# Moving weight loads, a half chunk's split and LayerNorm statistics to other steps of a planned two-layer kernel

## The chip, the cores and the metric

The kernel runs on one core of a Trainium2 chip (trn2). The metric is the device time of one execution in microseconds. A core has five engines that run side by side, each in its own order: TensorE (PE; its weight loads are shown apart as PEld), VectorE (DVE), ScalarE (ACT), GpSimd (POOL) and SyncE (SP), whose queue issues nearly all DMAs here.

## The reference

Two feed-forward layers with 4-bit weights stand around a long convolution (an S4 layer); each is added to its input.

```python
x = x + 0.5 * ffn(layernorm(x))
x = x + s4(layernorm(x))          # causal convolution over the last axis, plus D * u
x = x + 0.5 * ffn(layernorm(x))
# layernorm: (x - mean) / sqrt(var + 1e-5) over the last axis
# ffn: h = silu(x @ Wg) * (x @ Wu); return h @ Wd
# W[k, n] = scales[k // 128, n] * (w4[k, n] - (z4[k // 128, n] + 1)), eight 4-bit values to an int32
```

x is 2 x 1024 x 1024 in float32, so 2048 rows of 1024. The hidden width of the feed-forward layers is 2752, which is 21 chunks of 128 and a half chunk of 64.

## The kernel before, in words

**Jobs.** The 2048 rows are four blocks of 512 (four tiles of 128 rows each). A job is one feed-forward layer on one block, so there are eight, in the order `JOBS = [(0, 1), (1, 1), (0, 3), (1, 3), (2, 1), (3, 1), (2, 3), (3, 3)]`: block, then 1 for the first layer and 3 for the second. The convolution of a block (its LayerNorm has the number 2) is done during the up stage of the job that follows the block's first layer: in jobs 1, 2, 5 and 6. The block's next norm (number 3) follows there too.

**Stages and steps.** Each job has an up stage and a down stage. The up stage (`gate_up`, L727) multiplies the normalized, transposed rows with gate and up weights in eight waves of three or two chunks (the last wave has the half chunk as well), each wave over eight groups of 128 rows of weights: 64 steps, with 12, 8 or 10 matmuls (L753). Each product stays in a PSUM accumulator that is rescaled in place between two groups (`scaled`, L721 to L725), half of them by ScalarE and half by VectorE; after the last group `gated` (L778) makes silu(gate) * up, and GpSimd splits the result into a high and a low part (L785, L787). The down stage (`down`, L814) has two passes over 22 chunks: 44 steps of 8 matmuls (L825), with the same kind of rescaling; the last chunk of a pass, steps 21 and 43, is the half chunk, with 4. In job 0 ScalarE takes three of the four rescalings in every second down step. `back` (L843) then transposes the result and adds it to x, one half of the columns (512) at a time: the first half during the down stage, the second half in steps 0 to 3 of the next job's up stage.

**Weights.** In job 0 the 4-bit weights are turned into bytes first. For wave w, `fetch` and `fetch_zeros` load packed words and zero points (four DMAs of 128 or 192 KB, eight for the last wave, L514 and L521), `split` (L582) makes signed bytes in six VectorE operations (L575, L577, L579), and `dequantize` (L605) copies them in eight pieces on GpSimd (L608), each written to DRAM by a DMA (L609). All later steps load bytes from there, four steps ahead of their use (`load_bytes`, L685), and a cast three steps ahead turns them into matmul weights (`make_weights`: GpSimd L701, in job 0 for three steps of eight ScalarE L699). A wave's first load needs all eight writes of that wave. `first_weights` (L643) fixes at which steps of job 0 all of this is written.

**Order.** `fast` (L1420) writes the program job by job. Work that lies beside the matmuls is hung on steps: `at(up, s, f)` or `at(dn, d, f)` calls f at the start of a step, after the loads and casts of that step and before its matmuls. The framework's planner then orders each engine's instructions at compile time, and may run what is ready earlier than it was written. `in_order_of_writing(f, engines)` (L141) takes that freedom away: each instruction that f writes for the named engines is put behind the one written before it on that engine. `in_pieces` (L587) hangs a generator's pieces on a list of steps, with VectorE in order of writing.

**Norms.** `moments` (L176) runs BATCH_NORM_STATS2 on each half row (L187), an aggregate for each of four tiles (L190), and `guess` (L194, three small operations, a first value for 1/sqrt). `moments_by_tile` is the same as a generator: with `halves=True` a piece is one statistic, or one statistic with its aggregate, and the ninth is the guess. `deviations` (L206) refines with Newton's formula in ten small operations:

```python
for three in (3.0, 12.0, 768.0):
    nc.vector.tensor_tensor(e, r, r, ALU.mult)
    nc.vector.tensor_tensor(e, e, ve, ALU.mult)
    nc.vector.scalar_tensor_tensor(r, e, three, r, ALU.subtract, ALU.mult)
nc.vector.tensor_scalar(r, r, -factor / 8192, None, ALU.mult)
```

For job 1's rows this happens in the down stage of job 0: statistics pinned to steps 4 to 20, Newton to 21, normalization (L256) from 22 and turning (`turn_by_pool`, L236: transposes, a copy on ScalarE, a cast and a subtraction on GpSimd) from 24. For the norms 2 and 3 in jobs 1, 2, 5 and 6, `moments` and `deviations` are hung on single steps without an order: steps 4 and 5, and 27 and 28 (61 and 62 in job 1).

**The half chunk.** `gated_half` (L790) writes the high part of h (L802) and the low part (L804) of the 64-wide chunk. In jobs 1 to 7 GpSimd does this at down steps 1 and 2. In job 0 VectorE does it at once, at the end of the up stage.

## Time and profile before

| what | value |
|---|---|
| median of 3 runs | 2098.28 us (2097.29 to 2102.04) |
| the profiled execution: its time, and its span in the trace | 2097.59 us, 2095.8 us |
| TensorE busy, VectorE, ScalarE, GpSimd | 98%, 80%, 67%, 62% |
| granted TensorE clock | 0.998 |
| job 0, up stage and down stage | 176.7 us, 91.1 us |
| job 1, up stage and down stage | 193.0 us, 82.2 us |
| jobs 2, 5, 6, up stage | 188.3, 186.8, 186.8 us |
| jobs 3, 4, 7, up stage | 158.2, 158.3, 157.7 us |
| jobs 2 to 6, down stage | 80.5 to 80.6 us |

A stage's time is from its first matmul's start to the next stage's first, in the timeline of TensorE. All jobs have the same matmuls; the up stages of jobs 1, 2, 5 and 6 have the convolution's besides. In the lines of a timeline the columns are start in us, duration in us, engine, line of the program, operation, tiles written and read, their shapes, and the number of like instructions merged; in brackets stands the idle time before, and what ended it. In the chain of work that ended last they are start, duration, engine, tile and line. In a table of windows they are the window and its length, then the busy time of each engine with its number of instructions, the granted clock, the share of the DMA engines' time, and GB/s.

### The profile page before, as it was taken

Reading aid. Unit: us, or ns where it says so; the run is one execution under the profiler, and the core shown is the slowest. Engines: PE = TensorE matmul, PEld = TensorE weight load, DVE = VectorE, ACT = ScalarE, POOL = GpSimd, SP = SyncE. Lnnn points to the kernel's source line nnn. Section 1 sums busy time; section 2 is a strip of 40 time slices with the busy share of each in tenths; the row PEclk is TensorE's granted clock in tenths of the full one; section 3 lists DMA queues with packets and bytes.
Section 4 is the critical chain, followed back from the end, with each engine's and each line's share of the span. In section 5 each row is a group of like instructions: output and inputs, shape, how many; then the busy total and the mean of one; then the engine's idle time right before and its main releaser. Section 6 shows DMA issues by size and latency. Waiting matters only on the chain.

```text
span 2095.8 us, 30242 instructions
## 1 busy us (share of the span) xinstructions
PE 2054.6 (98%) x9556; PEld 1410.6 (67%) x9556; DVE 1671.5 (80%) x2749; ACT 1398.9 (67%) x2185; POOL 1291.6 (62%) x1688
## 2 busy tenths in 40 slices
PE   6999999999999999999999999999999999999998
PEld 4555775677776578655876568675686766866576
DVE  8888887778888877797778878878788787777776
ACT  6777777746655776667667776547765467667775
POOL 5867758657754577555955568455684546845542
PEclk9999999999999999999999999999999999999999
DMA  4324321113411126211441124111151111531111
GB/s 144 119 85 146 111 66 54 36 56 74 110 39 55 32 53 170 72 31 36 122 137 37 31 51 126 44 51 32 46 130 37 51 39 35 133 128 36 33 35 60
DMA packets 239719, 151.03 MB, mean 72 GB/s; under 512 B 98747, under 2 KB 226596, under 8 KB 239550
## 3 DMA queue, kind: packets, MB, share of 16 engines
q1 hardware_dynamic: 238246, 146.60, 24.7%
q8 instruction: 78, 1.28, 0.3%
q10 hardware_dynamic: 1016, 1.82, 0.2%
q14 instruction: 91, 0.75, 0.1%
q0 software_dynamic: 288, 0.59, 0.1%
HBM read 104.45 MB, written 25.50 MB: 62 GB/s over the span
## 4 chain that ended last, share of the span: by engine, by line
PE 92%; DVE 4%; DMA 1%; ACT 1%; issue 1%; POOL 0%; SPq 0%; ACTq 0%; DVEq 0%; POOLq 0%
PE pg L753 56%; PE po L825 29%; PE pc L1151 3%; PE pb L847 1%; PE pb L1151 1%; DVE pg L725 1%; PE st L230 1%; DMA b<-wq 1%; ACT g L780 0%; DVE po L725 0%; DVE x L256 0%; DMA x<-in_L_attn_u_dram 0%; POOL q L608 0%; DVE hf L783 0%; PE pt L230 0%
## 5 line engine op out<-in xcount | busy, mean ns | idle before, releaser
L723 ACT ACTIVATE pg<-pg,rat 128x512 f32<-128x512 f32 x1240 | 787.5, 661 | 418.1 <-PE pg L753 415.9
L725 DVE TENSOR_TENSOR pg<-pg,rat 128x512 f32<-128x512 f32 x1168 | 776.6, 693 | 159.3 <-PE pg L753 153.4
L753 PE MATMUL pg<-xTh,w_up 128*128 128x512 f32 x2752 | 840.5, 435 | 1.1 <-DVE pg L725 0.7
L753 PE MATMUL pg<-xTl,w_up 128*128 128x512 f16 x2752 | 716.7, 382 | 11.6 <-DVE pg L725 5.6
L701 POOL CAST w_up<-b 128x768 fp32r<-128x768 int8 (+2 forms) x490 | 378.0, 777 | 504.6 <-PE pg L753 405.7
L753 PEld LDWEIGHTS pg<-xTh,w_up 128*128 128x128 f32 x2752 | 518.3, 189 | 175.9 <-DVE pg L725 12.2
L723 ACT ACTIVATE po<-po,ratd 128x512 f32<-128x512 f32 x660 | 431.8, 661 | 164.7 <-PE po L825 164.1
L825 PE MATMUL po<-hl,w_down 128*128 128x512 f32 x1344 | 530.5, 397 | 3.7 <-DVE po L725 3.6
L825 PE MATMUL po<-hh,w_down 128*128 128x512 f32 x1344 | 521.2, 390 | 0.0
L725 DVE TENSOR_TENSOR po<-po,ratd 128x512 f32<-128x512 f32 x620 | 430.4, 698 | 113.3 <-PE po L825 109.1
L753 PEld LDWEIGHTS <-w_up 128*128 128x128 bf16 x2752 | 228.4, 99 | 330.3 <-issue 151.0
L701 POOL CAST w_down<-bd 128x512 fp32r<-128x512 int8 x352 | 218.4, 624 | 158.5 <-PE po L825 90.4
L825 PEld LDWEIGHTS po<-hl,w_down 128*128 128x128 f32 x1344 | 251.2, 188 | 73.3 <-DVE po L725 12.2
L825 PEld LDWEIGHTS po<-hh,w_down 128*128 128x128 f32 x1344 | 252.6, 188 | 49.0
L787 POOL TENSOR_TENSOR hl<-hf,hh 128x512 fp32r<-128x512 f32 x168 | 217.9, 1297 | 8.0
L783 DVE SCALAR_TENSOR_TENSOR hf<-pg,rat,g 128x512 f32<-128x512 f32 x168 | 123.2, 749 | 49.3 <-ACT g L780 40.4
L780 ACT ACTIVATE g<-pg,rat 128x512 f32<-128x512 f32 x168 | 111.0, 687 | 48.5 <-PE pg L753 32.8
L785 POOL CAST hh<-hf 128x512 fp32r<-128x512 f32 x168 | 106.1, 632 | 55.0 <-PE pg L753 31.0
L282 POOL TENSOR_TENSOR lo<-x,hi 128x512 f16<-128x512 f32 x48 | 62.2, 1296 | 0.0
L187 DVE BATCH_NORM_STATS2 stats<-x 128x6 f32<-128x512 f32 x88 | 60.0, 682 | 0.5
L280 POOL TENSOR_TENSOR mid<-hi,top 128x512 bf16<-128x512 f32 x48 | 56.4, 1174 | 0.0
L296 POOL TENSOR_TENSOR xTh<-turned 128x512 fp32r<-128x512 bf16 x48 | 55.9, 1165 | 0.0
(216 smaller groups left out, 1104.2 us busy)
## 6 DMA issues: line engine op xcount, KB each, us to landing
b<-wq SPq DMA_DIRECT2D x319, 96.0 KB
bd<-wdq SPq DMA_DIRECT2D x336, 64.0 KB
x<-in_L_attn_u_dram SPq DMA_DIRECT2D x30, 512.0 KB
b<-wq SPq DMA_DIRECT2D x128, 64.0 KB
xs<-x SPq DMA_DIRECT2D x16, 512.0 KB
x<-xs SPq DMA_DIRECT2D x16, 512.0 KB
out_dram<-x SPq DMA_DIRECT2D x12, 512.0 KB
b<-wq SPq DMA_DIRECT2D x64, 80.0 KB
```

Source lines behind the costliest of these rows:

```text
L187: nc.vector.bn_stats(stats[:, t, i, :], x[b][t][:, bass.ts(i, 512)])
L282: nc.gpsimd.tensor_tensor(lo[:, own], n[:, own], hi[:, own].bitcast(F32), ALU.subtract)
L701: nc.gpsimd.tensor_copy(t, b)
L723: nc.scalar.activation(dst, src, AF.Copy, scale=sc)
L725: nc.vector.tensor_tensor(dst, src, sc.to_broadcast([P, TB]), ALU.mult)
L753: nc.tensor.matmul(p, weights, (lo, hi)[k][:, g, :], start=(g == 0 and not done), stop=(g == GK - 1 and done), skip_group_check=True,)
L780: nc.scalar.activation(g, pg, AF.Silu, scale=rat[:, 2 * f, GK - 1 :])
L783: nc.vector.scalar_tensor_tensor(hf, pu, last, g, ALU.mult, ALU.mult)
L785: nc.gpsimd.tensor_copy(hi, hf)
L787: nc.gpsimd.tensor_tensor(lo, hf, hi.bitcast(F32), ALU.subtract)
L825: nc.tensor.matmul(ps[c], w[:, bass.ts(c, P)], part, start=(f == 0 and k == 0), stop=(f == NF - 1), skip_group_check=True,)
L1151: nc.tensor.matmul(dst, lhsT, rhs, start=start, stop=stop, skip_group_check=True)
```

## The change

Four things move. In job 0 the loads for the waves 4 to 7 are written two steps later, at steps 14, 22, 30 and 38, and wave 2's split and copies, with the load for wave 3, one step earlier. Job 0's half chunk is split in the down stage: its high part by ScalarE at step 6, its low part by VectorE at step 8. In job 0's down stage the statistics of job 1's rows come a step earlier and normalization and turning a step later, with Newton's operations in three pieces at steps 20, 21 and 22. All other statistics and Newton operations of the jobs are hung in pieces too, in order of writing on VectorE: norm 2 at steps 1 to 7, norm 3 at steps 14 to 28 (34 later in job 1), and Newton's steps for the first norm of blocks 2 and 3 at steps 27, 28 and 29 instead of 28.

```diff
         ln[b] = (mv, ve, r)
     def deviations(b, k, factor=1.0):
+        for r in deviations_in_pieces(b, k, factor):
+            pass
+        return r
+
+    def deviations_in_pieces(b, k, factor=1.0):
         mv, ve, r = ln.pop(b)
...
             nc.vector.tensor_tensor(e, r, r, ALU.mult)
             nc.vector.tensor_tensor(e, e, ve, ALU.mult)
             nc.vector.scalar_tensor_tensor(r, e, three, r, ALU.subtract, ALU.mult)
+            if three < 768.0:
+                yield r
         nc.vector.tensor_scalar(r, r, -factor / 8192, None, ALU.mult)
         for t in range(NT):
             ln[b, t] = (mv[:, t, 0:1], r[:, t : t + 1], k)
-        return r
+        yield r
     def normalized(b, t):
         m, r, k = ln[b, t]
...
         for w in range(1, len(WAVES)):
-            s0 = (0, 4, 8 * w - 15)[min(w, 3) - 1]
+            s0 = (0, 3, 8 * w - 15)[min(w, 3) - 1]
             steps = (0, 1, 2, 2, 3, 3) if w == 1 else range(6)
             in_pieces(at, [(up, s0 + d) for d in steps], lambda w=w: split(w))
             copies = {1: (2, 2, 3, 3, 3, 3, 3, 3), 2: (3, 3, 4, 4, 6, 6, 7, 7)}
             if 1 < w < len(WAVES) - 1:
                 both = lambda w=w: (fetch(w + 1), fetch_zeros(w + 1))
-                at(up, s0 + 3, lambda both=both: in_order_of_writing(both, ET.SP))
+                at(up, s0 + (3 if w == 2 else 5), lambda both=both: in_order_of_writing(both, ET.SP))
             for k, d in zip((0, 2, 4, 6, 1, 3, 5, 7), copies.get(w, (3, 3, 4, 5, 6, 6, 7, 8))):
                 at(up, s0 + d, lambda w=w, k=k: dequantize(w, k))
         s0 = len(STEPS) - 12
...
         both = hpool.tile([P, TB], F32R, tag="h", name=f"hb_{j}")
         h[WIDE] = (both,)
-        def split(e):
-            e.tensor_copy(both[high], hf[high])
-            yield
+        def split():
+            if j:
+                nc.gpsimd.tensor_copy(both[high], hf[high])
+            else:
+                nc.scalar.copy(both[high], hf[high])
+            yield
+            e = nc.gpsimd if j else nc.vector
             e.tensor_tensor(both[low], hf[high], both[high].bitcast(F32), ALU.subtract)
-        half_split[j] = split(nc.gpsimd if j else nc.vector)
-        if j == 0:
-            for _ in half_split[j]:
-                pass
+        half_split[j] = split()
+
     half_split = {}
     yT = {}
...
                     at(up, t, lambda t=t: back(pb, 1, t))
                 if pk == 1:
                     late = 34 if j == 1 else 0
-                    at(up, 4, lambda: moments(pb, 2))
-                    at(up, 5, lambda: deviations(pb, 2))
+                    steps = [(up, s) for s in (1, 2, 2, 3, 3, 4, 4, 5, 5)]
+                    in_pieces(at, steps, lambda: moments_by_tile(pb, 2, halves=True))
+                    steps = [(up, s) for s in (6, 7, 7)]
+                    in_pieces(at, steps, lambda: deviations_in_pieces(pb, 2))
                     s4x, s4n = {}, {}
                     def norm(t):
...
                         at(up, late + 10 + 4 * t, lambda t=t: swap(t))
                         at(up, late + 12 + 4 * t, lambda t=t: conv(t))
                         at(up, late + 13 + 4 * t, lambda t=t: next(parts[t], None))
-                    at(up, late + 27, lambda: moments(pb, 3))
-                    at(up, late + 28, lambda: deviations(pb, 3, LIFT))
+                    steps = [(up, late + s) for s in (14, 15, 18, 19, 22, 23, 26, 26, 27)]
+                    in_pieces(at, steps, lambda: moments_by_tile(pb, 3, halves=True))
+                    steps = [(up, late + s) for s in (27, 28, 28)]
+                    in_pieces(at, steps, lambda: deviations_in_pieces(pb, 3, LIFT))
                     def save():
                         for t, dst in enumerate(saved(pb)):
...
                 if ak == 1:
                     at(up, 55 if j == 0 else 6, lambda: load_x(ab, rows_of(u, ab)))
                     if j == 0:
-                        steps = [(dn, d) for d in range(4, 22, 2)]
+                        steps = [(dn, d) for d in range(3, 21, 2)]
                         in_pieces(at, steps, lambda: moments_by_tile(ab, 1, halves=True))
-                        newton = lambda: deviations(ab, 1, LIFT)
-                        at(dn, 21, lambda: in_order_of_writing(newton, ET.DVE))
+                        steps = [(dn, d) for d in (20, 21, 22)]
+                        in_pieces(at, steps, lambda: deviations_in_pieces(ab, 1, LIFT))
                     else:
                         steps = [(up, s) for s in range(18, 27)]
                         in_pieces(at, steps, lambda: moments_by_tile(ab, 1, halves=True))
-                        newton = lambda: deviations(ab, 1, LIFT)
-                        at(up, 28, lambda: in_order_of_writing(newton, ET.DVE))
+                        steps = [(up, s) for s in (27, 28, 29)]
+                        in_pieces(at, steps, lambda: deviations_in_pieces(ab, 1, LIFT))
                 turns = {}
                 def turning(t):
...
                 for t in range(NT):
                     for half in range(2):
-                        d, where = ((22 + 4 * t + 2 * half, dn), (3 * t + half, dn))[min(j, 1)]
+                        d, where = ((23 + 4 * t + 2 * half, dn), (3 * t + half, dn))[min(j, 1)]
                         if j > 1:
                             d, where = 31 + 2 * t + half, up
                         piece = lambda t=t, half=half: normalize(ab, t, half)
...
                     if j == 0:
                         for half in range(2):
                             piece = lambda t=t, half=half: turn_by_pool(ab, t, half)
-                            at(dn, 24 + 4 * t + 2 * half, piece)
+                            at(dn, 25 + 4 * t + 2 * half, piece)
                         continue
                     late = (12, 13) if t == NT - 1 else (13, 17)
                     for d in (1, 2, 3, 5, 6, 7, 9) + late:
                         piece = lambda t=t: turning(t)
                         piece = lambda piece=piece: in_order_of_writing(piece, ET.Pool, ET.SP)
                         at(dn, 2 + 9 * t + d, piece)
-            for d in (1, 2) if j else ():
+            for d in (1, 2) if j else (6, 8):
                 piece = lambda j=j: next(half_split[j], None)
-                at(dn, d, lambda piece=piece: in_order_of_writing(piece, ET.Pool))
+                engines = (ET.Pool,) if j else (ET.Activation, ET.DVE)
+                at(dn, d, lambda piece=piece, e=engines: in_order_of_writing(piece, *e))
             o, gap = (27, 3) if j == 0 else (21, 4)
             at(dn, o, lambda: load_x(b, rows_of(u, b) if k == 1 else saved(b)))
             for t in range(NT):
```

## The prediction

> **What bounds the kernel.** I read the page first, then the chain that ended last in order of time, then the timelines of TensorE, VectorE and the SP queue around each place where that chain leaves TensorE.
>
> ```profile
> span 2095.8 us, 30242 instructions
> PE 2054.6 (98%) x9556; PEld 1410.6 (67%) x9556; DVE 1671.5 (80%) x2749; ACT 1398.9 (67%) x2185; POOL 1291.6 (62%) x1688
> ```
>
> TensorE sets the end, but 98% hides short stalls, since matmul ends are modelled. So I counted the matmul starts step by step. A quiet step of a three-chunk wave (job 3, steps 4 to 30) takes 2.70 us for 12 matmuls, a quiet down step 1.83 us for 8. What a step takes beyond that, less its transposes and convolutions (0.11 us for each transpose), is stall. Jobs 2 to 7 have almost none: at most 0.7 us at step 33, 1.4 us more in job 2. Job 0 has some 17 us in its up stage and 7 in its down stage; job 1 some 4. Three of the stalls lie where the change works.
>
> **Stall 1**, 3.1 us before job 0's step 16 (75.4 to 78.7 us). The chain:
>
> ```profile
> 72.41 4.06 DMA b<-wq
> ...
> 76.54 0.46 ACT w_up L699
> ...
> 77.28 0.83 ACT w_up L699
> 78.11 0.59 ACT g L780
> ...
> 78.74 4.02 PE pg L753 x17
> ```
>
> ACT's queue stood at the cast of step 17's weights, waiting for their load; behind it stood the SiLU that frees an accumulator for step 16. The SP queue shows why the load was late:
>
> ```profile
> 69.27 0.32 SPq L685 DMA_DIRECT2D b<-wq  x1
> 69.64 0.42 SPq L514 DMA_DIRECT2D raw<-_L_ffn_gate_qweight_dram  x1
> 70.11 0.43 SPq L514 DMA_DIRECT2D raw<-in_L_ffn_up_qweight_dram  x1
> 70.64 1.23 SPq L521 DMA_DIRECT2D z<-z_dram  x2
> 71.91 0.46 SPq L609 DMA_DIRECT2D wq<-q  x1
> 72.41 0.43 SPq L685 DMA_DIRECT2D b<-wq  x1
> ```
>
> Wave 4's four loads (written at step 12) stand ahead of it: 2.3 us of issue, and 4.06 us to landing where the load at 47.28 took 1.87.
>
> **Stall 2**, 2.4 us in job 0's down steps 1 and 2 (1.5 and 0.9; jobs 2 to 7 show 0.3 and 0.1 there). VectorE splits the half chunk, although down step 21 is its first use:
>
> ```profile
> 201.45 1.70 DVE L802 CAST hb<-hf_half 64x512 fp32r<-64x512 f32 x1
> 203.18 0.70 DVE L725 TENSOR_TENSOR po<-po,ratd 128x512 f32<-128x512 f32 x1
> 203.91 0.91 DVE L804 TENSOR_TENSOR hb<-hf_half,hb 64x512 fp32r<-64x512 f32 x1
> ```
>
> **Stall 3**, 1.7 us in job 0's down step 23: guess and Newton, ten small operations pinned at step 21, push the two y and the next po back.
>
> ```profile
> 242.10 0.64 DVE L197 TENSOR_SCALAR ve<-mv 128x4 f32<-128x4 f32 x1
> ...
> 245.20 0.68 DVE L725 TENSOR_TENSOR y<-po,ratd 128x512 f32<-128x512 f32 x1
> ...
> 247.75 0.69 DVE L725 TENSOR_TENSOR po<-po,ratd 128x512 f32<-128x512 f32 x1
> ```
>
> **The skill.** (1) The Trainium skill, "Perfetto Trace Analysis", Tensor Engine Instruction (MATMUL, LD_WEIGHTS), says that ACT, DVE and GPSIMD are strict FIFO; stall 1 agrees, a SiLU waited 3.2 us behind a cast. (2) "DMA: Bandwidth & Descriptors", Queues, rings and completion order: each DMA engine consumes descriptors in ring order, so a load stands behind what was issued before it; 4.06 against 1.87 us agrees. (3) "SBUF — State Buffer", SBUF: two separate sides: DVE and GpSimd can lock one shared port pair. The cast of 1.70 us on VectorE, 0.61 us on POOL in the other jobs, fits that. (4) "Perfetto Trace Analysis", Optimizing Scalar/DVE Operations: if Vector isn't saturated but causes bubbles, breaking up instructions may help. That condition decides the last part:
>
> ```profile
> 569.40:589.40 20.00, 20.00 (x94) 12.35 (x92) 19.41 (x44) 12.84 (x21) 5.61 (x7) 1.00 0.13 35
> 838.20:858.00 19.80, 19.80 (x95) 12.39 (x93) 15.23 (x25) 12.87 (x21) 5.64 (x7) 1.00 0.36 131
> ...
> 569.40:589.40 20.00, 1.96 (x3) 1.00 0.13 35
> 530.00:566.00 36.00, 2.74 (x4) 1.00 0.39 89
> ```
>
> The first pair is every engine in steps 1 to 7 of job 2 and of job 3 (third figure: VectorE); the second pair is BATCH_NORM_STATS2 alone, in steps 1 to 7 of job 2 and in the down stage before. Job 2's VectorE is full at 19.41 of 20 us without stalling TensorE, because four of the eight statistics, those on first halves of x, ran a stage earlier than written.
>
> **The parts.**
> *Wave loads.* Wave 4's loads go behind those of steps 17 and 18. These two issue some 2.2 us earlier and land after some 1.9 us instead of 4.06, so the cast is ready by 72.5, before its turn. Stall 1 goes: **-3.1**. The loads of steps 19 and 20 then stand behind the four instead, landing near 78.5; step 19 starts at 84, so this is covered. The raw words land near 78, the split asks at 81 (84.5 now, less the gain). Waves 5 to 7: SP runs 2.5 to 3 steps ahead of TensorE, so 13 us or so are left before each split, 8 for wave 7; nothing. Each of these moves takes four DMAs past two b loads and up to four writes of copies on SP; no other engine's queue holds them. Wave 2 a step earlier: its split and copies only move, and its copies may use POOL's 3.6 us idle before 49.27 (gain up to 1.0); but wave 3's loads now precede the load of step 11, issued at 49.71 now. Near 52.4, with 4 us to landing, it would hold POOL's cast (53.47) to 56; step 11 starts at 60.7. I take 0, with -1.0 and +2.5 as ends.
> *Half chunk.* Off VectorE's queue go 1.70 and 0.91 us. Of 2.0 us excess in steps 1 and 2, I take 1.6 back; the pinned split of the down weights is late next. At step 6 ACT gets a copy of 64x512, not shown before: between VectorE's slot of 0.6 and the 0.66 us of ACT's 128x512 scaling. ACT has three scalings in an even step, 1.82 us of some 2.0, so it delays them: +0.2. VectorE's subtraction at step 8 waits for that copy, two steps old by then; it takes 0.7 to 0.9 us where VectorE is 86% busy (27.75 of 32.1 us in down steps 5 to 19): +0.1. Sum **-1.3** (-2.0 to +0.3).
> *Job 0's down stage.* Six of ten Newton operations move ahead of the y, guess a step earlier; the y no longer wait some 0.9 us: **-0.9** (-1.7 to +0.3). Normalization and turning go a step later with all that they issue: four transposes on TensorE, a copy on ACT, a cast and a subtraction on POOL each. The transposes cost the same in any step (these steps show 0.4 us each, four times 0.11, and nothing more); the last POOL split ends near 285, and job 1's first matmul at 290 is the first to need it.
> *Statistics and Newton after a norm, jobs 1, 2, 5, 6.* Pinned to steps 1 to 5, the four first-half statistics can't run in the down stage. Each now waits for the residual's addition written before it, behind it stand VectorE's scalings of that step, and TensorE's next step waits for those. VectorE's issue pitch for one is 0.60 us (568.51 to 569.11), so 2.4 us come into windows with 0.6 us free: 1.8 late. A scaled accumulator is needed eight matmuls (1.8 us) after its last one, and scaling takes 0.7, so TensorE bears 1.1 of lateness. Some 0.7 to 1.3 us a job are stall; I take 1.0 in jobs 2, 5 and 6. Job 1 has 1.6 us free (18.90 of 20.5) and ACT takes one scaling of every second step: 0.3. Sum **+3.3**, bounds 0 and 12 (below 0 isn't excluded by Newton's spreading, but job 2 has no stall left there).
> *Statistics before the second norm, and Newton at 27 to 29.* One operation a step at steps that convolutions lengthen; where job 3 has one a step pinned now (steps 18 to 26) no step stalls. **0**, -1 to +1.5.
> Sum: -3.1 - 1.3 - 0.9 + 3.3 = -2.0. The profiled execution took 2097.59 us, so 2095.6; the median of the runs is 0.7 above it, so **2096.3**.
>
> **Rivals.**
> *Pieces slip in for nothing* (0.35): the planner puts scalings between the pieces, lateness stays within 1.1 us. For it: VectorE at 97% doesn't stall TensorE now. Sum -5.3: 2093.0.
> *The pinned pieces become the wait* (0.19), slower. Jobs 1, 2, 5, 6, steps 2 to 5: two statistics and an aggregate are 1.35 us, with the residual's addition 1.95, ahead of a scaling that has 1.1. If the pieces always go first, five statistics (3.0 us) a job come through: +12, net +6.7: 2105.0. It decides from 1.1 us of lateness at step 3. Against it: an aggregate waits for its statistics, and a scaling can pass there.
> *Step 11's load* (0.04) holds POOL: +2.5 on the main sum, 2098.8.
> *The wave loads do nothing* (0.05): the planner leaves another transfer or a POOL copy before step 17's load, and stall 1 stays: 2099.4.
> The main case has 0.37.
>
> **The numbers.** About 0.2% (4.2 us) is what a measurement can tell from no change. Faster by more, below 2094.1: most of the first rival and a little of the main case, 0.37. Slower, above 2102.5: the second rival and the tails of the last two, 0.21. Within: 0.42. Range 2088.5 to 2105: down to the first rival with the good ends of waves and half chunk, up to the second. The main case alone: 2093 to 2100.
>
> **What would show it.** Right: no wait of TensorE near 75 us; job 0's down steps 1, 2 and 23 within 0.5 us of 1.83; no statistics of jobs 1, 2, 5, 6 in the down stage; TensorE waits for VectorE's pg scaling in steps 3 to 6 of jobs 2, 5 and 6, some 1 us each. Wrong: those jobs unchanged at 188.3 and 186.8 us of up stage (then the first rival), or longer by 3 (the second); a first job not some 5 us shorter.

## The result, and the profile after

The change makes the kernel slower: 2111.84 us, median of 5 runs (2109.6 to 2116.75), against 2097.29 us for the kernel before on the same chip (5 runs, 2094.4 to 2102.04). The ratio is 1.007, 95% interval 1.0051 to 1.009. The prediction had 2096.3 us, range 2088.5 to 2105; the result lies above the range, beyond even the slower rival's 2105.0. The profiled execution took 2109.6 us.

From the page of the kernel after: span, busy times, and the shares of the chain that ended last; the line below them is that of the kernel before.

```profile
span 2107.8 us, 30251 instructions
PE 2058.8 (98%) x9556; PEld 1407.9 (67%) x9556; DVE 1679.1 (80%) x2748; ACT 1400.5 (66%) x2186; POOL 1286.4 (61%) x1688
PE 87%; DVE 9%; DMA 1%; issue 1%; ACT 1%; POOL 0%; SPq 0%; ACTq 0%; DVEq 0%; POOLq 0%
...
PE 92%; DVE 4%; DMA 1%; ACT 1%; issue 1%; POOL 0%; SPq 0%; ACTq 0%; DVEq 0%; POOLq 0%
```

But for two operations of the half chunk, one of which is now ScalarE's, the engines do the same work as before; only the order is new. The first two lines hardly show the loss: TensorE is again 98% busy, VectorE 80%. The third shows it. In the kernel before the chain has VectorE at 4%; now it has 9%. The chain's time on VectorE is also time in which TensorE keeps pace with it, so this isn't the size of the loss, but it says which engine to read. The stages say where (us, from each stage's first matmul to the next stage's first):

| stage | before | after | difference |
|---|---|---|---|
| job 0 up | 176.7 | 173.8 | -2.9 |
| job 0 down | 91.1 | 95.7 | +4.6 |
| job 1 up | 193.0 | 197.6 | +4.6 |
| job 1 down | 82.2 | 83.6 | +1.4 |
| job 2 up | 188.3 | 191.0 | +2.7 |
| jobs 5 and 6 up | 186.8, 186.8 | 188.6, 188.5 | +1.8, +1.7 |

Everything else, the time before the first matmul included, is some 1.6 us shorter, 0.6 of it in job 7's up stage. Jobs 0 and 1 differ between kernels even where no edit touches them. Over the kernels below that leave the stage as it was, job 0's up stage takes 175.6 to 181.1 us, its down stage 91.1 to 93.1, mostly 92 to 92.9, and job 1's up stage 191.2 to 194.2. So of job 0's 4.6 us in the down stage some 3 are the edits', and in job 1 the steps have to be read: a stall of 1.3 to 1.6 us at step 24 and one of 1.0 us at step 45 come and go with no edit near them. The kernel before has the first, the kernel after the second. What the change costs job 1 stands at steps 9 and 10: by step 11 it is 4.8 us late.

The window of job 2's steps 1 to 7, with every engine (third figure: VectorE), then BATCH_NORM_STATS2 alone in this window and in the 36 us up to it (some 4 us later against the stages than in the prediction):

```profile
576.70:596.70 20.00, 20.00 (x94) 11.55 (x92) 20.00 (x42) 13.60 (x22) 5.56 (x7) 1.00 0.11 30
...
576.70:596.70 20.00, 5.36 (x8) 1.00 0.11 30
541.00:577.00 36.00, 0.00 (x0) 1.00 0.37 86
```

All eight statistics now stand in the up stage, none in the down stage, and VectorE went from 19.41 to 20.00 us of 20. Although five more of its instructions there are statistics, it has two instructions fewer (42 instead of 44): it is behind. The first line below is the guess in the kernel before; the rest is VectorE's timeline after, then GpSimd's, then TensorE's:

```profile
581.41 0.77 DVE L197 TENSOR_SCALAR ve<-mv 128x4 f32<-128x4 f32 x1
...
590.63 0.69 DVE L187 BATCH_NORM_STATS2 stats<-x 128x6 f32<-128x512 f32 x1
...
592.52 0.71 DVE L197 TENSOR_SCALAR ve<-mv 128x4 f32<-128x4 f32 x1
...
602.59 0.79 DVE L219 SCALAR_TENSOR_TENSOR r<-e,r 128x4 f32<-128x4 f32 x1
...
603.91 0.73 DVE L222 TENSOR_SCALAR r<-r 128x4 f32<-128x4 f32 x1
...
605.16 0.80 DVE L230 TENSOR_SCALAR xn<-x,mv,r 128x1024 f32<-128x1024 f32 x1
...
602.54 0.83 POOL L708 CAST w_up<-b 128x768 fp32r<-128x768 int8 x1
603.33 1.28 POOL L794 TENSOR_TENSOR hl<-hf,hh 128x512 fp32r<-128x512 f32 x1
...
605.29 0.49 PE L760 MATMUL pg<-xTh,w_up 128*128 128x512 f32 x1 [0.51 <-DVE pg L732]
606.01 1.09 PE L237 MATMUL st<-ident,xn 128*128 128x128 f32 x8 [0.22 <-DVE xn L230]
```

VectorE's timeline has no idle time in brackets from 577 to 606. The guess (L197) comes 19.8 us after the job's first matmul instead of 15.9, and the first tile's normalization ends after 33.2 us instead of 24.1. TensorE loses nothing up to the start of step 9; then 0.4 us at step 9 and 1.5 at step 10 are stall, besides the 0.9 us of the tile's transposes, which stood in step 9 before. What it waits for is first a rescaling (0.51 us), then the normalization (0.22 us).

The way there is not a plain backlog. Counted in the order in which they run, VectorE's rescalings in job 2 are up to 1.4 us later than in the kernel before during steps 1 to 6, but only 0.2 us around the end of wave 0. What stays late is Newton. In the kernel before its last operation ends 23.1 us after the job's first matmul; now eight of its ten stand in steps 8 to 10, where GpSimd is busy splitting the products of wave 0. There five of them take 0.66 to 0.79 us instead of 0.15, and each ends within 0.03 us of a GpSimd instruction's end (602.59 + 0.79 and 602.54 + 0.83; 603.91 + 0.73 and 603.33 + 1.28). In guess and Newton together this waiting, what an operation takes beyond 0.16 us, comes to 3.4 us, 1.4 in the kernel before. Then the rescalings are up to 2.1 us late, and TensorE waits.

The three stalls of job 0. **Stall 1** is gone from step 16; the chain shows what is left, 2.1 us at step 14:

```profile
71.65 2.10 DMA b<-wq
...
73.85 0.40 ACT w_up L706
...
74.59 0.66 ACT pg L730
```

The load for step 17 is issued at 69.42 us instead of 72.41, and its cast starts at 71.56 instead of 76.54. Now ScalarE waits for the load of step 18, which takes 2.10 us to land. **Stall 2** has moved. VectorE's timeline at the start of the down stage:

```profile
198.17 0.83 DVE L582 TENSOR_SCALAR rawd<-rawd 88x512 int32<-88x512 int32 x1
199.04 0.70 DVE L732 TENSOR_TENSOR po<-po,ratd 128x512 f32<-128x512 f32 x1
199.65 0.93 DVE L584 TENSOR_TENSOR rawd<-rawd,zd 88x1024 uint16<-88x1024 uint16 x1
200.50 1.50 DVE L582 TENSOR_SCALAR rawd<-rawd 88x512 int32<-88x512 int32 x1
```

Where the half chunk was, the pinned split of the down weights (88 rows) moved up at once: steps 1 to 3 lose 0.6, 2.3 and 1.6 us, before 1.5, 0.9 and 0.1. The split's first five operations take 0.82 to 1.50 us at this place, where in the kernel before they took 0.41 to 0.72. These durations differ between kernels with the same order of work: with the half chunk left in place the three steps lose 2.3 to 3.8 us, so the kernel before, at 2.5, is near the low end. **Stall 3** stays at 1.8 us at step 23 (1.7 to 3.1 in the kernels that leave it alone), and the chain names another owner: not Newton but the second pass's weights, copied, written and loaded (`241.40` to `250.13`).

```profile
241.40 1.72 POOL qd L644 x3
243.14 1.59 DMA wdq<-qd
...
248.33 1.80 DMA bd<-wdq
250.13 0.72 PE po L834 x2
```

### The profile page after: what moved, and what is told of

Same layout as the page of the kernel before. It is cut to its first block, busy times and chain, and to the rows that moved or that the text cites. A ratio compares the mean times of both kernels' runs of the same rounds, so it can differ in the third digit from the quotient of the medians.

```text
span 2107.8 us, 30251 instructions
## 1 busy us (share of the span) xinstructions
PE 2058.8 (98%) x9556; PEld 1407.9 (67%) x9556; DVE 1679.1 (80%) x2748; ACT 1400.5 (66%) x2186; POOL 1286.4 (61%) x1688
## 3 DMA queue, kind: packets, MB, share of 16 engines
q8 instruction: 78, 1.28, 0.2%
## 4 chain that ended last, share of the span: by engine, by line
PE 87%; DVE 9%; DMA 1%; issue 1%; ACT 1%; POOL 0%; SPq 0%; ACTq 0%; DVEq 0%; POOLq 0%
PE pg L760 52%; PE po L834 29%; DVE pg L732 4%; PE pc L1160 3%; PE pb L1160 1%; PE pb L856 1%; DVE stats L187 1%; PE st L237 1%; DMA b<-wq 1%; DVE x L263 1%; DVE hf L790 0%; DVE po L732 0%; DVE x L858 0%; DMA x<-in_L_attn_u_dram 0%; DVE even L584 0%
## 5 line engine op out<-in xcount | busy, mean ns | idle before, releaser
L760 PE MATMUL pg<-xTh,w_up 128*128 128x512 f32 x2752 | 853.0, 437 | 6.6 <-DVE pg L732 5.3
L760 PE MATMUL pg<-xTl,w_up 128*128 128x512 f16 x2752 | 724.8, 382 | 10.2 <-DVE pg L732 6.2
L834 PEld LDWEIGHTS po<-hl,w_down 128*128 128x128 f32 x1344 | 251.8, 188 | 76.6 <-DVE po L732 14.5
```

Source lines behind the costliest of these rows:

```text
L760: nc.tensor.matmul(p, weights, (lo, hi)[k][:, g, :], start=(g == 0 and not done), stop=(g == GK - 1 and done), skip_group_check=True,)
L834: nc.tensor.matmul(ps[c], w[:, bass.ts(c, P)], part, start=(f == 0 and k == 0), stop=(f == NF - 1), skip_group_check=True,)
```

## The experiments

Unless said otherwise a kernel is the one before with one edit, "excess" is what a step takes beyond a quiet one, its transposes included, and stage times are from the profiled execution. The numbers in brackets after a ratio are its 95% interval.

### Each part alone

**The wave loads.** Edit: the two lines of `first_weights` in the change.

> The kernel before with the move of the wave loads alone. Theory (each part acts where it is written): job 0's up stage falls from 176.7 to about 174 us, the stall before step 16 goes down from 3.1 us and the 1.2 us in steps 18 and 19 goes; every later stage keeps its length to 0.3 us; the whole is some 2.5 us shorter, ratio 0.999. Rival (the parts act on each other through the planner's order): job 0's up stage does not fall, or job 0's down stage rises from 91.1 us by more than 1 us though nothing in it is edited.

Measured: ratio 0.9991 (0.9982 to 1.0), which no change at all just fits too. Job 0's up stage takes 174.3 us; the stall before step 16 went from 3.1 to 0.1 us, with 2.1 at step 14. That the edit gains is clearer in the steps: over steps 0 to 31 job 0's excess is 13.5 to 14.0 us in the four kernels that have it and 15.1 to 17.6 us in all others.

**The half chunk.** Edit: `split` of the half chunk and the steps (6, 8) of job 0.

> The kernel before with the half chunk's split in the down stage alone. Theory: the stall is not removed but handed on. The two operations stood in VectorE's queue ahead of the pinned split of the down weights (six operations at down steps 0 to 3); without them these six start some 6 us earlier, while GpSimd still splits the last chunks, take up to 1.5 us each and stand ahead of the first rescalings: excess in down steps 0 to 3 rises from 2.7 to about 4.7 us, job 0's down stage from 91.1 to about 93 us. Rival (the prediction's step): excess falls by 1.3 to 2 us, to about 89.5 us.

Measured: 1.0008 (1.0001 to 1.0015). Excess of steps 0 to 3: 0.2, 0.7, 2.3, 0.1 (before 0.2, 1.5, 0.9, 0.1). The stall was handed on from step 1 to step 2, in VectorE's timeline as in the kernel after. The sum is within what these steps vary by (2.3 to 3.8 us).

**Job 0's down stage.** Edit: statistics from step 3 on, Newton in pieces at 20, 21, 22, normalization and turns one step later.

> The kernel before with the change of job 0's down stage alone (statistics a step earlier, Newton in three pieces, normalization and turning a step later). Theory: the Newton operations no longer hold step 23, but the weights of the second pass do (chain of copy, write, load), so the excess there stays near 1.7 us, and normalization a step later costs 1 to 2.6 us in steps 24 to 40: down stage 92 to 93.7 us. Rival (the prediction's step): step 23's excess falls to 0.8, down stage 90.2 us.

Measured: 1.001 (1.0003 to 1.0017), down stage 94.8 us. Excess 2.0 us at step 3, 1.4 at step 23, and a new 1.7 at step 30. The first isn't this edit's: two kernels that leave job 0's start of the down stage alone have it too.

**Norm 2.** Edit: statistics at steps 1 to 5, Newton at 6, 7, 7, both in order of writing.

> The kernel before with the pieces of norm 2 alone (statistics pinned to steps 1 to 5, Newton to 6 and 7, jobs 1, 2, 5, 6). Theory: all that jobs 5 and 6 lost comes back here: up stages 188.5 us instead of 186.8, job 2 some 190.1, job 1 some 197; the excess lies at step 10 (TensorE waits for the normalized tile's transposes), not at steps 3 to 6; the whole is 9 us longer, ratio 1.004. Rival: norm 3's pieces share the loss; then jobs 5 and 6 stay within 1 us of 186.8.

Measured: 1.0058 (1.0041 to 1.0075): most of the loss. Jobs 5 and 6 take 188.6 and 188.9 us; the stall is at steps 9 and 10, as in the kernel after, not in steps 3 to 6. Job 1 has an excess of 4.3 us at step 9 and 1.4 at step 10.

**Norm 3.** Edit: statistics at steps 14 to 27, Newton at 27, 28, 28, and Newton of the first norm at 27, 28, 29.

> The kernel before with the pieces of norm 3 and of Newton at steps 27 to 29 alone. Theory (each part acts where it is written): jobs 5 and 6 stay within 0.3 us of 186.8; job 2 is some 1 us longer (189.4), where the check of the indices fills VectorE too; job 1's down stage 83.6 us instead of 82.2. Rival: no stage changes by more than 0.3 us, and what the changed kernel loses there comes from the parts together.

Measured: 1.002 (1.0014 to 1.0027). Job 1's down stage 83.6 us (0.3 at step 1, 0.6 each at steps 5 and 8), job 2's step 26 1.6 us instead of 0.7; jobs 5 and 6 unchanged. The five parts sum to -0.9 + 0.8 + 1.0 + 5.8 + 2.0 = +8.7 parts in a thousand; the whole is +7.0 (5.1 to 9.0).

### What in norm 2 costs

**Statistics alone; Newton alone; the swap later.** First: the statistics in pieces, Newton free.

```diff
-                    at(up, 4, lambda: moments(pb, 2))
+                    steps = [(up, s) for s in (1, 2, 2, 3, 3, 4, 4, 5, 5)]
+                    in_pieces(at, steps, lambda: moments_by_tile(pb, 2, halves=True))
```

> The kernel before with norm 2's statistics pinned to steps 1 to 5, but Newton hung on step 5 without an order, as before. Theory (two delays add up against a slack): in jobs 2, 5 and 6 tile 0's normalization ends 24.1 us after the job's first matmul in the kernel before, the transposes that need it start at 29.3, so there are 5.2 us of slack; pinned statistics delay guess and Newton by some 4 us, less than that; up stages of jobs 5 and 6 stay within 0.5 us of 186.8. Rival (statistics alone carry the loss): 188.5 us. In job 1 some +1 us over 191.2 to 193.0.

Second: `moments` free, Newton in pieces at 6, 7, 7.

> The kernel before with norm 2's Newton pinned in pieces to steps 6, 7, 7, statistics without an order, as before. Theory (two delays add up against a slack of 5.2 us): the pieces alternate with rescalings and take some 5 us longer, tile 0's normalization ends near 29 us after the job's first matmul, jobs 5 and 6 lose 0 to 0.8 us (186.8 to 187.6). Job 1 carries most of its loss here, since the third gated product of wave 0 stands behind Newton and the pole table: 194 to 196 us. Rival (Newton's pieces alone carry the loss): 188.5 us in jobs 5 and 6.

Third: norm 2's part whole, with the transposes (`swap`) and the convolution one step later.

> Norm 2's pieces as in the changed kernel, nothing else of the change, and in jobs 1, 2, 5 and 6 the transposes of each tile and its convolution one step later (11, 13, 14 instead of 10, 12, 13, and so on by fours). Theory (TensorE waits in its own order for the late normalization): one step gives 2.7 us, the wait before step 10 in jobs 2, 5 and 6 falls from 2.8 to about 0.3 us, and their up stages return to within 0.5 us of 186.8; job 1, where the transposes are 34 steps away, stays at 196.4. Rival (VectorE's lateness itself holds TensorE through the rescalings): up stages of jobs 5 and 6 stay near 188.5.

Measured: 1.0047 (1.003 to 1.0064), 1.0006 (0.9997 to 1.0015), 1.0057 (1.004 to 1.0075). Jobs 5 and 6 take 188.5, then 187.5 and 187.4, then 188.3 and 188.4 us. So in jobs 2, 5 and 6 the statistics carry the loss, and Newton's pieces alone cost 0.6 to 0.8 us a job. In job 1 the two go together: by step 11 it is 2.4 us late with the statistics alone, 0.3 us early with Newton's pieces alone, and 4.8 us late with both. My theory that TensorE waits in its order for a late swap fell: with the swap a step later the excess of step 10, transposes included, only went from 2.4 to 2.0 us. The edit put the transposes just three matmuls later on TensorE, since the planner had already placed them late; but the wait for the normalization is gone there, and the 0.51 us for a rescaling is still the same. So it is the rescalings that hold TensorE.

**Where the statistics stand.** Two reasons were left: that pinning costs wherever it is done, or that this place costs. Both kernels pin all eight statistics: the first halves in the down stage, one step after the piece of the residual they read, the second halves in the up stage.

```diff
+            if k == 1:
+                steps = [(dn, o + 6 + gap * t) for t in range(NT)]
+                steps += [(next_up, s) for s in (2, 3, 4, 5)]
+                in_pieces(at, steps, lambda b=b: moments_by_tile(b, 2, halves="apart"))
```

> The kernel before with one edit: the eight norm-2 statistics of each job stay fixed in VectorE's order of writing, but the four of the first halves are written into the previous down stage, one step after the piece of the residual that they read, where VectorE has idle time between rescalings; only the four of the second halves and their aggregates stand in up steps 2 to 5. Newton's steps are free as before. Theory (amount: 2.4 us of first-half statistics added to a VectorE that is busy 19.4 of 20.0 us in steps 1 to 7): nothing is added there, so jobs 5 and 6 come back from 188.5 us to 186.8 to 187.1 us in the up stage, job 2 to 188.3 to 188.6, job 1 to 191 to 193.5; the down stages stay 80.6 us; ratio 0.9995 to 1.0015. Rival (fixing the statistics in the order of writing costs, wherever their first halves stand, since second halves and aggregates at fixed places hold up rescalings): jobs 5 and 6 stay at 187.8 to 188.6 and the ratio at 1.003 to 1.005. Second rival (the statistics become a wait in the down stage): up stages as before, but down stages 1 and 4 to 5 longer by 0.5 us or more each.

Then `(1, 2, 3, 4)` for the second halves, nothing else:

> As the kernel with the first halves' statistics fixed in the previous down stage, but the four second halves with their aggregates one step sooner, in up steps 1 to 4, each directly after the piece of the residual that it reads. Theory (what is left of the loss, 3.0 us in job 1 and 0.7 us in job 2, is lateness: the second halves end at 309 us there, where they end at 303 us in the kernel before, and the Newton steps and pole-table operations behind them come down on the third gated product of wave 0): job 1 takes 191 to 193.5 us in the up stage instead of 196.0, job 2 188.2 to 188.6 instead of 189.0, jobs 5 and 6 186.7 to 187.0; ratio 0.9993 to 1.0008. Rival (the fixed order itself: any statistic or aggregate fixed in steps 1 to 8 holds up rescalings and pole-table operations, wherever it stands): job 1 stays at 195 us or more, job 2 at 188.9 or more; ratio 1.0015 to 1.003.

Measured: 1.0021 (1.0014 to 1.0028), then 1.0 (0.9991 to 1.0008). With the first halves back in the down stage, jobs 5 and 6 take 187.1 us, job 2 189.0, but job 1 still 196.0, outside that theory's 191 to 193.5. One step sooner they take 186.7, 188.3 and 192.3 us. The second kernel's windows, as those shown above, and its statistics of first halves alone:

```profile
569.40:589.40 20.00, 20.00 (x94) 12.36 (x93) 19.61 (x45) 12.81 (x21) 5.58 (x7) 1.00 0.13 35
...
530.00:566.00 36.00, 2.74 (x4) 1.00 0.39 89
```

All eight statistics are pinned, VectorE is full at 19.61 us, and TensorE loses nothing in jobs 2, 5 and 6. So pinning as such is free here; two things in the place cost. The amount: four first halves in a full window, 1.4 of the 1.7 us in jobs 5 and 6, 1.0 of 1.7 in job 2. The lateness: second halves two steps behind the residual instead of one, the rest there and, in job 1, what the statistics cost: by its step 11 it is 2.4 us late with all eight in the up stage, 3.1 with the second halves a step too late, 0.8 in the last kernel. (Of the 3.7 us between 196.0 and 192.3, 1.6 are the stall at step 24 that comes and goes.) Both act through Newton: its last operation ends 31.9 us after the job's first matmul in job 5 of the kernel after, 25.8 and 23.1 us in these two, and 23.1 in the kernel before.

Job 1's VectorE also makes the tables for the convolution in these steps. In the kernel after, and below it one line of GpSimd:

```profile
319.09 1.13 DVE L219 SCALAR_TENSOR_TENSOR r<-e,r 128x4 f32<-128x4 f32 x1
...
320.91 1.40 DVE L932 SCALAR_TENSOR_TENSOR s_sin<-s_cos,s_vc,s_sin 128x512 f32<-128x512 f32 x2
322.24 0.73 DVE L790 SCALAR_TENSOR_TENSOR hf<-pg,rat,g 128x512 f32<-128x512 f32 x1
...
318.93 1.28 POOL L794 TENSOR_TENSOR hl<-hf,hh 128x512 fp32r<-128x512 f32 x1
```

The third line is wave 0's third gated product, which frees accumulators for the next wave. Newton and the table's operation stand before it; its two fellows were done at 316. Newton's last eight operations take 4.7 us in all, where at 0.16 us each they would take 1.3; the one shown ends when GpSimd's subtraction does (320.22 and 320.21).

**The whole change with norm 2's statistics so placed.**

> The whole change with one part of it placed anew: norm 2's first-half statistics are fixed in the previous down stage, one step after the residual's piece, and the second halves with their aggregates in up steps 1 to 4; Newton's pieces stay at steps 6, 7, 7. Theory (late statistics of norm 2 are the change's main loss, 5 to 6 parts in a thousand, and Newton's pieces alone cost 0.6): jobs 5 and 6 take 186.8 to 187.5 us in the up stage instead of 188.6 and 188.5, job 2 189 to 190 (with 0.9 from norm 3's pieces), job 1 191 to 193.5 instead of 197.6; what is left is 1.2 (whole less norm 2's part) plus 0.6, with the parts' own sum at 3.5: ratio 1.0010 to 1.0038. Rival (the parts hold each other up: with statistics out of the way, Newton's late pieces or norm 3's take over the wait): ratio 1.004 or more, job 1 at 195 us or more.

Measured: 1.0031 (1.0019 to 1.0043). Jobs 5 and 6 187.5 us, job 1 192.8, job 2 190.5 (0.5 over what was expected). The statistics' place alone is 7.0 less 3.1, 3.9 parts in a thousand or some 8 of the 14.5 us; both figures have about 1 to 2 parts of uncertainty. What is left fits the other parts: -0.9, 0.8, 1.0, 2.0 and Newton's 0.6 sum to 3.5.

### Job 0's down stage

**The down-weight split spread behind the half chunk.** The half chunk's edit, and

```diff
                 steps = [when(max(0, n - d)) for d in (4, 3, 3, 2, 1, 0)]
+                if n == 16:
+                    steps = [(dn, d) for d in (1, 2, 2, 3, 3, 4)]
```

> The kernel before with two edits: the half chunk's two pieces of job 0 in the down stage (steps 6 and 8, as in the change), and the six pieces of the 88-row down-weight split moved from around the first down steps to down steps 1, 2, 2, 3, 3, 4. Theory (after the half chunk leaves, the fixed split of the down weights stands ahead of the first rescalings and hands the stall on from step 1 to step 2): with the split spread later, the excess of down steps 0 to 4, 3.3 us with the half chunk alone and 2.7 us in the kernel before, falls to 1.0 to 2.0 us, so job 0's down stage takes 89.5 to 91.5 us and the ratio is 0.9990 to 1.0000. Rival (the split's end, not its place, is what counts: step 16's matmuls of the second half need its result, or the stall comes with the first rescalings themselves): excess of steps 0 to 4 stays at 2.5 us or more, or moves to steps 4 to 8, and the ratio stays at 1.0000 to 1.0015.

Measured: 0.9996 (0.9988 to 1.0005). Excess of steps 0 to 4: 0.2, 0.3, 0.0, 0.2, 0.8, sum 1.5 us where the half chunk alone leaves 3.4; the down stage 89.7 us, shorter than in any kernel that leaves it alone. The place of the split was the next wait. In the whole the gain isn't clear of no change.

**Newton alone, the normalization alone, the two together.** The three kernels take one or both of the change's edits at steps 20 to 25.

> The kernel before with one edit: in job 0's down stage only Newton's steps of the next job come in three pieces at down steps 20, 21 and 22 instead of whole at step 21; statistics and normalization stay where they are. Theory (the stall at down step 23 belongs to the chain that copies, writes and loads the second pass's down weights, with Newton beside it): the excess at step 23 stays at 1.2 to 1.8 us, job 0's down stage stays at 91.1 to 92.8 us, ratio 0.9997 to 1.0006; so the loss of the down-stage part as a whole (+2 to +3 us) is that of the normalization one step later. Rival (Newton whole at step 21 makes the stall, and the later normalization spoilt its gain): the excess at step 23 falls to under 0.8 us, the down stage to 90.0 to 91.3 us, ratio 0.9992 to 0.9998.

> The kernel before with one edit: in job 0's down stage only, the eight half normalizations and the eight turns by GpSimd one step later (from steps 23 and 25 on instead of 22 and 24). Theory (the loss of the down-stage part comes from here[...]): job 0's down stage takes 93.5 to 95 us with excess of 0.5 us or more in more steps from 24 to 36 than before; ratio 1.0005 to 1.0018. Rival (the statistics one step earlier make it, where they meet the down-weight split in steps 3 to 5): the down stage stays at 91 to 92.8 us, ratio 0.9996 to 1.0005.

> The kernel before with two edits in job 0's down stage: Newton's pieces at down steps 20, 21 and 22, and normalization and turning one step later; the statistics stay at steps 4 to 20. Each of the two alone left the time unchanged, while all three edits of this stage cost 1.0 part in a thousand. Theory (the two together cost: a normalization one step later follows directly on the last Newton piece and both meet the split of the second pass's weights on VectorE): a stall of 1 us or more at down step 30, which only the whole part had, the down stage at 93.5 to 95 us, ratio 1.0003 to 1.0015. Rival (the statistics one step earlier are the missing term): no stall over 0.6 us at step 30, the down stage at 91 to 93 us, ratio 0.9994 to 1.0004.

Measured: 0.9994 (0.9985 to 1.0003), 1.0 (0.9992 to 1.0009), 0.9996 (0.9988 to 1.0005). Step 23 loses 1.8, 2.1 and 1.3 us, where kernels that leave it alone lose 1.7 to 3.1; the stage takes 93.8, 91.6 and 91.5 us, the first with 3.7 us in steps 1 to 3, which no edit touches, so Newton alone stays within what job 0 varies by. With Newton in pieces the chain at that step still runs over VectorE, over Newton's pieces and the down-weight split; in the kernel after it runs over the weights, so the stall has two owners, and which one shows differs. Norm_later's theory fell, and so did that of the pair: neither has the 1.7 us at step 30. In the kernel with the whole part it is one normalization, in VectorE's timeline and then every engine in that window (fifth figure: GpSimd):

```profile
259.35 0.71 DVE L263 TENSOR_SCALAR x<-x,mv,r 128x512 f32<-128x512 f32 x1
...
263.45 2.54 DVE L263 TENSOR_SCALAR x<-x,mv,r 128x512 f32<-128x512 f32 x1
...
262.70:266.00 3.30, 2.87 (x15) 2.07 (x13) 3.16 (x3) 2.79 (x6) 3.30 (x6) 1.00 0.13 29
```

It takes 2.54 us where its fellows take 0.53 to 0.91, while GpSimd runs six instructions without a gap. The Trainium skill, "SBUF — State Buffer", SBUF: two separate sides, has DVE and GpSimd lock one shared port pair; this fits it, but a busy GpSimd isn't enough (the fellow at 259.35 had one beside it too and took 0.71 us), and the 2.0 us more are longer than any one GpSimd instruction there (at most 1.28 us), so what makes this one so long isn't shown. By elimination the statistics one step earlier shift GpSimd's copies into that gap; that edit wasn't tried alone, so it is argued, not shown.

### The gains together

The wave loads, the half chunk, and the split spread, nothing else.

> The wave loads of the change, the half chunk's pieces of the change, and the 88-row down-weight split at down steps 1, 2, 2, 3, 3, 4; nothing of the other edits. Theory (the two gains lie in different stages of job 0 and add up: 2 to 3 us in its up stage, 1 to 3 us in its down stage): job 0 takes 173.5 to 175 us and 89 to 90.5 us, the excess of down steps 0 to 4 stays under 1.8 us; ratio 0.9978 to 0.9992, so this one beats both kernels. Rival (the wave loads' gain is taken back where the split now stands, or job 0's spread from kernel to kernel is as large as the gain): ratio 0.9992 to 1.0003.

Measured: ratio 0.9985 (0.9976 to 0.9993), so it is faster than both kernels by a little. The down stage is 89.5 us, as expected. The up stage was not, in this profile: 179.7 us, with 3.7 at step 53, where the chain waits 6.76 us for one write of copied weights (wq). That wait isn't this kernel's own: step 53 has an excess of 0.4 to 2.6 us in the others, and a write of 6.69 us stands in the chain of the kernel with norm 2's statistics alone. This execution, 2099.65 us, was the longest of thirteen.

## Why the prediction was wrong, step by step

- **Wave loads, -3.1: right in the stall, too large in the net.** The stall before step 16 is gone; the next wait, 2.1 us at step 14, wasn't named. Alone the edit measured -0.9 parts in a thousand, 1.9 us. (The 3.2 us that the prediction gives for the SiLU are ScalarE's idle time before the cast.)
- **Half chunk, -1.3: wrong in its net.** The step named what is late next, "the pinned split of the down weights", but priced it at 0.4 of 2.0 us. It took everything: measured +0.8 part in a thousand (0.1 to 1.5). The two moved operations themselves were sized right: 0.62 us on ScalarE, 0.69 on VectorE. With the split spread over later steps the first five down steps lose 1.2 us less than before, so there the term would have been about right.
- **Job 0's down stage, -0.9: wrong.** Stall 3 was read as Newton's, and in the kernel before the chain does run over Newton. But the copy, write and load of the next weights end at nearly the same time. Newton in pieces and the later normalization, alone or together, measured no change, so the term should have been near 0; the whole part cost +1.0 part in a thousand, 2 us.
- **Norm 2, +3.3: right that it costs, wrong in where and how much, and this made the miss.** The step that failed is "behind it stand VectorE's scalings of that step, and TensorE's next step waits for those": 1.8 us late, less 1.1 of slack, taken as 1.0 a job in steps 3 to 6. That lateness came (up to 1.4 us), but it was absorbed: TensorE lost nothing there, and by the end of wave 0 the rescalings were back to 0.2 us. At nothing stood what the statistics push back in their turn: guess and Newton, 3.9 us later. They came to stand beside GpSimd's splits and waited for them 2.0 us more than before, and TensorE lost 1.8 us at steps 9 and 10. That 1.8 is also the prediction's figure before the slack is taken off looks like chance, since the wait is another one. The term for job 1, 0.3 from "1.6 us free", was the largest error: it is 4.8 us late by step 11, since what counted was not the sum of its window but one product behind Newton and the tables. With 1.8 in three jobs and 4.8 in job 1 the step gives 10.2; norm 2 alone measured 5.8 parts in a thousand, 12.2 us (8.6 to 15.7). That the place of the statistics is the cause is shown by moving them. The link over GpSimd is read from the traces; no kernel here moves GpSimd's splits alone.
- **Norm 3, 0 (-1 to +1.5): wrong.** 2.0 parts in a thousand, 4.2 us. Its profile locates only 2.3 of them: 1.4 us in job 1's down stage, where late Newton steps hold job 2's normalization, and 0.9 in job 2. The step took steps 18 to 26 of job 3 as its model; in job 1 the pieces stand 34 steps later, right before the down stage whose normalizations need them.
- **The signs.** No statistics of norm 2 in the down stages: seen. TensorE waiting in steps 3 to 6: not, it waits at steps 9 and 10. No wait near 75 us: not, one step earlier there are 2.1 us. Job 0's down steps 1, 2 and 23 within 0.5 us: not, they lose 0.6, 2.3 and 1.8. Job 0 some 5 us shorter: it is 1.7 longer.
- **The rivals.** The slower one, "the pinned pieces become the wait", comes nearest, but it too has the wait in steps 2 to 5, and its 3.0 us a job is too much for jobs 2, 5 and 6 and too little for job 1. "Step 11's load" did come about in part: GpSimd's cast for that step starts at 59.39 us instead of 53.47, but TensorE lost no more than 0.5 us by it. The Trainium skill, "Perfetto Trace Analysis", Optimizing Scalar/DVE Operations, offers breaking up instructions for an engine that isn't saturated. The prediction read that condition off the window, 19.41 of 20 us, and rightly charged a loss instead of a benefit; this case's trace agrees with the page as far as it goes, since pieces added to a full window cost 1.8 us a job.

## What to carry to other kernels

Before work is pinned to steps, look where it runs while it is free: a planner may have taken it out of a full window, and the pin must name that earlier place. Where an engine has no idle time, work added to it pushes back what is written behind it: ask what that later work will then stand beside. Here the rescalings caught up within a few steps, and the small operations behind them ran into another engine's burst. When a stall is taken away, price the next pinned work behind it as if it moved up at once, and look for a second chain that ends at the same time.

## What wasn't expected of the hardware

- VectorE's operations of 128x4 elements took 0.14 to 0.17 us whenever no GpSimd instruction ran beside them: 1928 of them over the traces of these 18 kernels, without an exception. Beside a GpSimd instruction 470 of 898 took more than 0.3 us, twice 1.13 us in job 1's steps 8 and 9 of the kernel after, and each of the 470 ended within 0.06 us after the end of a GpSimd instruction. So a chain of small dependent operations on VectorE is best placed where GpSimd has gaps.
- One normalization of 128x512 took 2.54 us instead of 0.54 beside a busy GpSimd.
- In job 0's up stage the last 80 KB writes of wave 7's copied weights stand on the SP queue among four loads of 512 KB each. In the last kernel one such write took 6.76 us, and the load behind it 2.83 us, where the load in stall 1 took 2.10. From the last of these writes to the load that needs them it is 4.6 us in the kernel after and 5.3 in the one before, so it is slow in these too.
